# A layernorm, attention and FFN kernel in split precision: narrow matmuls joined, layernorm shared with GpSimd, eight idle transposes at the branch

## The chip, the cores and the metric

The kernel runs on one core of a Trainium2 chip. TensorE (PE) multiplies matrices into PSUM, an accumulator memory of eight banks; VectorE (DVE), ScalarE (ACT) and GpSimd (POOL) do elementwise work[...]; SyncE (SP) issues DMAs, as ACT and POOL also do. Each engine works through its own queue in order, and semaphores tie the queues together. The metric is the device time of one execution in microseconds, lower is better.

## What is computed

Four sequences of 512 tokens with 512 features pass a layernorm. Its output goes through causal attention with 16 heads of 128, and through a gated FFN whose three weight matrices hold -1, 0 and 1. The results are multiplied and added to x.

```python
xn = _layernorm(x)                                   # x: 4 x 512 x 512
q = einsum("bpd,hde->bphe", xn, W_Q) + b_Q           # k and v alike
scores = where(causal, einsum("bqhe,bkhe->bhqk", q, k) / sqrt(128), -1e5)
z = einsum("bkhe,bhqk->bqhe", v, softmax(scores))
s = einsum("bqhe,hed->bqd", z, W_O) + b_O
hdn = silu(einsum("th,ih->ti", xn, gate_w) * gate_s) * (einsum("th,ih->ti", xn, up_w) * up_s)
g = silu(einsum("ti,hi->th", hdn, down_w) * down_s)  # 1408 wide inside
out = x + s * g
```

## The kernel before

**Split precision.** Matmuls run in fp32r, whose operands are rounded. Each operand is therefore kept as a high part (ACT copies it with rounding) and a low part (the value minus the high part), a `Split`. A product is three matmuls into one PSUM bank: high x low, high x high, low x high (`mm3`).

**Stages.** A start loads x and the first weights, normalizes batch 0 and transposes it (128 x 128 transposes on TensorE). Then 64 heads run in an order of groups of two heads (`HG = 2`), the four batches inside each group. After them, one value says whether the FFN weights are exact in the high part alone, every engine branches on it, and `ffn` runs.

**One head `n`**, in the order in which its instructions are issued on every engine (the order is written out by hand):

1. `softmax`: scores of this head in three PSUM tiles, row maximum on DVE, exponent on ACT, reciprocal on DVE, scaling of p on GpSimd.
2. two `project_v` (first head of a pair) or two `project_out` of the group before (second head): `fill` over the first half of the tokens.
3. `turn_p`: p is transposed in 32 x 32 blocks on DVE, written to DRAM and read back with its blocks in place.
4. `split_p`: the p of the head before is split, in two halves, on ACT (high, `pth`) and DVE (low, `ptl`). In the first heads it comes before step 2.
5. `split_pending`: weights that are due are split, high on ACT, low on GpSimd. Weights are loaded through four `raw` buffers; later loads wait on the ACT queue until GpSimd has finished with a buffer.
6. `project`: q and k of the next head, each evacuated by ACT (high) and DVE (low).
7. `attend`: z of the head before, from twelve matmuls of 512, 128, 384 and 256 columns in three rounds. Key tile j of 128 reaches only query tiles j and later, so the last key tile has 128 columns. z is evacuated by ACT (`zT.hi`) and DVE (`zT.lo`).
8. `fill` over the second half of the tokens.

In heads 0, 2 and 4 the next batch is also normalized: statistics and `ln_normalize` on DVE, then in step 8 four `ln_transpose` (four transposes, a copy to the high part on ACT) and `ln_low` (DVE).

PSUM has three banks for score and transpose tiles (`ps_st`) and five for all else (`ps_mm`), reused in turn. `warm_up` issues 24 transposes of the identity at the start. The line in `softmax` that reads the high and low part of k side by side is

```python
nc.tensor.matmul(two, qT.hi[:, :P], kT.both[:, :, :P], start=True, stop=False)
nc.tensor.matmul(where[0], qT.lo[:, :P], kT.hi[:, :P], start=False, stop=True)
```

Of the kernel before, what the change touches and what calls it, by code (L numbers as in the profile page):

```python
# [10 lines left out]
F32 = mybir.dt.float32  # L11
F32R = mybir.dt.float32r
# [10 lines left out]
BIG = 3.0e38  # L23
WARM = 24
LOW_BITS = (1 << 12) - 1
# [17 lines left out]
def kernel(  # L43
# [46 lines left out]
    def mm3(ps, a, b, first, last):  # L90
        nc.tensor.matmul(ps, a.hi, b.lo, start=first, stop=False)  # L91
        nc.tensor.matmul(ps, a.hi, b.hi, start=False, stop=False)  # L92
        nc.tensor.matmul(ps, a.lo, b.hi, start=False, stop=last)  # L93


    with ExitStack() as at:
# [35 lines left out]

        def split_w(dst, raw):
            nc.scalar.copy(dst.hi, raw)
            nc.gpsimd.tensor_tensor(dst.lo, raw, dst.hi32, ALU.subtract)

# [12 lines left out]

        def split_pending(n):  # L150

            for due, dst, raw in [p for p in pending if p[0] <= n]:
                split_w(dst, raw)
            pending[:] = [p for p in pending if p[0] > n]
# [46 lines left out]

        def warm_up():

            junk = ps_st.tile([P, NT, P], F32, name="warm", tag="st")
            for k in range(WARM):
                nc.tensor.transpose(junk[:, k % NT, :], ident, ident)

        def ln_normalize(b, t):
            xt = x_in.pop((b, t))
            mv, sd = ln_of.pop((b, t))  # L210
            rstd = small.tile([P, 1], F32, name="rstd")
            nc.vector.reciprocal(rstd, sd)
            xn = lnp.tile([P, D], F32, name="xn")
            nc.vector.tensor_scalar(xn, xt, mv[:, 0:1], rstd, ALU.subtract, ALU.mult)
            xn_of[b, t] = xn

        def ln_transpose(b, t):
            xn = xn_of.pop((b, t))
            pool, tag = ((ps_st, "st"), (ps_mm, "mm"))[t % 2]
            tr = pool.tile([P, ND, P], F32, name="tr", tag=tag)  # L220
            for c in range(ND):
                nc.tensor.transpose(tr[:, c, :], xn[:, ts(c, P)], ident)
            to = xnT[b][:, :, ts(t, P)]
            nc.scalar.copy(to.hi, tr)
            lo_of[b, t] = lambda: nc.vector.tensor_tensor(to.lo, tr, to.hi32, ALU.subtract)  # L225

        def ln_low(b, t):
            lo_of.pop((b, t))()
# [3 lines left out]
        def project_v(g, b, t):  # L232
            ps = ps_mm.tile([P, HG * E], F32, name="psv", tag="mm")
            for c in range(ND):
                mm3(ps, xnT[b][:, c, ts(t, P)], wv[g][:, c, :], c == 0, c == ND - 1)
            v = weight(vp, [P, HG * E], f"v{g}_{b}_{t}", "v")
            nc.scalar.copy(v.hi, ps)
            nc.vector.tensor_tensor(v.lo, ps, v.hi32, ALU.subtract)
            v_of.setdefault((g, b), []).append(v)

        def project(b, h, w, bias, name, parts=1):

            ps = ps_mm.tile([P, S], F32, name="ps" + name, tag="mm")
            both = qkp.tile([P, 2, S], F32R, name=name, tag=name)
            q = Split(both[:, 0, :], both[:, 1, :])
            q.both = both
            for k in range(parts):
                at_ = ts(k, S // parts)
                for c in range(ND):
                    mm3(ps[:, at_], w[:, c, :], xnT[b][:, c, at_], c == 0, c == ND - 1)  # L250
                yield
                nc.scalar.activation(  # L252
                    q.hi[:, at_], ps[:, at_], AF.Identity, bias=bias[:, h : h + 1]
                )
                nc.vector.scalar_tensor_tensor(  # L255
                    q.lo[:, at_], ps[:, at_], bias[:, h : h + 1], q.hi32[:, at_],
                    ALU.add, ALU.subtract,
                )
            yield q
# [85 lines left out]

        def split_p(raw):
            pt = weight(pp, [P, NS, P], "pt", "pt")
            half = NQ // 2
            for k in range(0, NQ, half):
                src = raw[:, k : k + half].rearrange("p b (s i) -> p b s i", i=Q)  # L350

                def dst(part):
                    return part[:, :, k * Q : (k + half) * Q].rearrange(
                        "p s (b i) -> p b s i", i=Q
                    )

                nc.scalar.copy(dst(pt.hi), src)  # L357
                nc.vector.tensor_tensor(dst(pt.lo), src, dst(pt.hi32), ALU.subtract)  # L358
            return pt

        def transpose_p(of):

            pt = weight(pp, [P, NS, P], "pt", "pt")
            pairs = [(j, t) for j in range(NT) for t in range(j, NT)]
# [10 lines left out]

        def attend(h, pt, vs):
            z = ps_mm.tile([P, NT, P], F32, name="z", tag="mm")


            todo = []  # L380
            for part, other in (("hi", "hi"), ("lo", "hi"), ("hi", "lo")):
                for j in (0, NT - 1, 1, 2):
                    v = getattr(vs[j], part)[:, ts(h % HG, E)]
                    p_ = getattr(pt, other)[:, slot[j] : slot[j] + NT - j, :]
                    todo.append((z[:, j:, :], v, p_))
            for k, (o, v, p_) in enumerate(todo):
                nc.tensor.matmul(o, v, p_, start=k == 0, stop=k == len(todo) - 1)  # L387
            zT = weight(zp, [P, NT, P], f"z{h}", "z")

            bias = bv_sb[:, h : h + 1]  # L390
            nc.scalar.activation(zT.hi, z, AF.Identity, bias=bias)
            nc.vector.scalar_tensor_tensor(zT.lo, z, bias, zT.hi32, ALU.add, ALU.subtract)
            return zT
# [67 lines left out]
        with tc.manual_schedule():  # L461
            nc.gpsimd.memset(eps, EPS)
            for t in range(NT):
                load_x(0, t)
            prepare_qk(0, -4, -3)
            prepare_v(0, -2)
            bq_sb, bk_sb, bv_sb, gs_sb, us_sb = small_const()
# [7 lines left out]
            make_causal_mask(nc, mask[:, S - P :], mask_val=IGNORE / SCALE)  # L475
            ln_stats(0, [0])
            ln_sd(0, [0])
            ln_stats(0, [1])
            ln_sd(0, [1])
            ln_normalize(0, 0)  # L480
            split_pending(-4)
            ln_transpose(0, 0)
            ln_stats(0, [2])
            ln_sd(0, [2])
            ln_normalize(0, 1)
            ln_low(0, 0)
            split_pending(-3)
            ln_transpose(0, 1)
            ln_low(0, 1)
            q_of = project(0, 0, wq[0], bq_sb, "q", 2)  # L490
            k_of = project(0, 0, wk[0], bk_sb, "k", 2)
            next(q_of)
            split_pending(-2)
            prepare_qk(1, -1)
            ln_stats(0, [3])
            ln_sd(0, [3])
            ln_normalize(0, 2)
            ln_transpose(0, 2)
            ln_normalize(0, 3)
            ln_low(0, 2)  # L500
            ln_transpose(0, 3)
            next(k_of)
            ln_low(0, 3)
            next(q_of)
            next(k_of)
            split_pending(-1)
            table(AF.Exp)
            qT = next(q_of)
            kT = next(k_of)
            for t in range(NT):  # L510
                load_x(1, t)
            bo_bc = load_const(b_o.broadcast_to([P, D]), [P, D], "bo_bc")
            ds_bc = load_const(down_s.broadcast_to([P, D]), [P, D], "ds_bc")
            project_v(0, 0, 0)

# [5 lines left out]
            def attend_last(before, pt):  # L521
                g, b, i = before
                zs.setdefault((g, b), []).append(attend(g * HG + i, pt, v_of[g, b]))

            for n, (g, b, i) in enumerate(heads):
# [21 lines left out]
                if n == 1:  # L547
                    pt = split_p(raw)
                of = softmax(qT, kT)
                if n > 1 and early:  # L550
                    pt = split_p(raw)
                look()
# [4 lines left out]
                if not early:  # L557
                    pt = split_p(raw)
                split_pending(n)
# [24 lines left out]
                if nxt is not None:  # L584
# [7 lines left out]
                    if ln_next:  # L592
                        for t in range(NT):
                            ln_normalize(b + 1, t)
                if nxt is not None:
# [6 lines left out]
                if ln_b is not None and n > 0:  # L602
                    ln_sd(ln_b, range(NT))
                    table(AF.Exp)
                if ln_next:
                    fill(range(half, NT))
                    for t in range(NT):
                        ln_transpose(b + 1, t)
                        ln_low(b + 1, t)
                    if b + 2 < B:  # L610
                        for t in range(NT):
                            load_x(b + 2, t)
# [10 lines left out]
            last = (NG - 1, B - 1)  # L623
            zs[last].append(attend(H - 1, pt, v_of[last]))
            for t in range(NT):
                project_out(*last, t, zs[last])


# [175 lines left out]
```

## Time and profile before

| what | us |
|---|---|
| three runs, median (lowest to highest) | 1222.99 (1222.97 to 1223.63) |
| the profiled execution | 1222.41 |
| its span, first to last instruction | 1220.6 |
| first score matmul | 20.58 |
| last matmul of the attention starts | 972.68 |
| first FFN matmul starts | 974.00 |
| last matmul ends, near | 1213.9 |

Busy time by stretch, in us:

| stretch | length | PE | DVE | ACT | POOL |
|---|---|---|---|---|---|
| 20.58 to 95.48, first heads | 74.90 | 72.55 | 65.35 | 44.81 | 14.11 |
| 228.98 to 243.90, one head, n = 14 | 14.92 | 14.92 | 12.46 | 7.43 | 5.61 |
| 243.90 to 258.57, the next | 14.67 | 14.67 | 12.32 | 8.06 | 8.71 |
| 258.57 to 964.80, the other heads | 706.23 | 706.23 | 523.87 | 323.01 | 180.28 |
| 973.08 to 1213.90, the FFN | 240.82 | 239.90 | 96.49 | 68.77 | 45.90 |

A row of the timeline reads: start in us, length in us, engine, line, operation, output<-inputs, shape (partitions x elements), count, and in brackets the idle time before it and what ended it. `L387` is line 387 of the kernel before. PE stands for the matmuls, PEld for the loads of their stationary operand. A row of waits reads: engine, tile and line that waited, who was waited for, total us, times, longest. A row by stretch reads: stretch, length, then busy time and count of PE, PEld, DVE, ACT and POOL, then the granted TensorE clock, the share of the DMA engines and GB/s.

### The profile page before, as it was taken

How to read it: one execution, taken by the hardware profiler on the slowest of the kernel's cores; microseconds unless marked ns; L12 is line 12 of the kernel's file. 1: busy time of each engine (PE TensorE's matmuls, PEld its weight loads, DVE VectorE, ACT ScalarE, POOL GpSimd, SP SyncE). 2: the span in 40 equal slices, each digit the busy share in tenths (PEclk: the TensorE clock that was granted, in tenths of full speed). 3: DMA queues.
4: the chain of work that ended last, by engine and by line, in shares of the span. 5: the costliest groups of instructions: out<-in, count | busy, mean ns of one | idle time of the engine just before them, and what ended most of it. 6: DMA issues, size and time to landing. Idle time of an engine off the chain costs nothing.

```text
span 1220.6 us, 18887 instructions
## 1 busy us (share of the span) xinstructions
PE 1206.5 (99%) x6514; PEld 1052.7 (86%) x6514; DVE 827.1 (68%) x2044; ACT 525.3 (43%) x1169; POOL 301.7 (25%) x433
## 2 busy tenths in 40 slices
PE   8999999999999999999999999999999999999997
PEld 8888888888888888888888888888888888888886
DVE  6897777777777777777877676767677533434343
ACT  5654444444445445444544454445444342323231
POOL 4212321232123213321412141214121341212010
PEclk9999999999999999999999999999999999999999
DMA  4454456656665667566655565555544893627241
GB/s 161 138 175 147 145 165 206 206 179 190 190 207 174 203 198 218 181 208 192 211 182 173 178 189 175 177 185 173 173 156 156 272 317 93 207 87 213 80 147 38
DMA packets 117912, 215.55 MB, mean 177 GB/s; under 512 B 13232, under 2 KB 45744, under 8 KB 117808
## 3 DMA queue, kind: packets, MB, share of 16 engines
q1 hardware_dynamic: 74016, 134.51, 34.4%
q10 hardware_dynamic: 29376, 53.26, 14.2%
q0 software_dynamic: 14416, 26.48, 7.9%
q8 instruction: 53, 0.87, 0.3%
q14 instruction: 51, 0.42, 0.1%
HBM read 135.17 MB, written 79.04 MB: 175 GB/s over the span
## 4 chain that ended last, share of the span: by engine, by line
PE 95%; DVE 3%; ACT 1%; DMA 0%; issue 0%; SPq 0%; DVEq 0%; ACTq 0%
PE z L387 10%; PE pd L667 7%; PE pg L667 7%; PE pu L667 7%; PE pso L91 5%; PE psv L91 5%; PE pso L92 5%; PE pso L93 5%; PE psv L93 5%; PE psv L92 5%; PE psq L91 5%; PE psq L92 5%; PE psq L93 5%; PE psk L91 5%; PE psk L92 5%; PE psk L93 5%
## 5 line engine op out<-in xcount | busy, mean ns | idle before, releaser
L316 POOL TENSOR_SCALAR p<-p,rtot 128x512 f32<-128x512 f32 (+3 forms) x256 | 148.2, 598 | 675.1 <-DVE rtot L315 675.1
L312 ACT ACTIVATE p<-p,nmax 128x512 f32<-128x512 f32 (+3 forms) x256 | 140.9, 552 | 147.3 <-DVE nmax L298 147.3
L358 DVE TENSOR_TENSOR ptl<-ptr,pth 128x640 fp32r<-128x640 f32 x126 | 133.7, 1099 | 1.4 <-ACT pth L357 1.4
L330 DVE STREAM_TRANSPOSE sq<-p 128x256 f32<-128x256 f32 x378 | 113.3, 361 | 0.0
L298 DVE CUSTOM_DVE_ANT_0 p<-sc,mask 128x512 f32<-128x512 f32 (+2 forms) x192 | 96.5, 552 | 0.3 <-PE sc L93 0.3
L252 ACT ACTIVATE k<-psk,consts 128x512 fp32r<-128x512 f32 (+1 forms) x65 | 44.2, 681 | 108.7 <-PE psk L93 108.6
L252 ACT ACTIVATE q<-psq,consts 128x512 fp32r<-128x512 f32 (+1 forms) x65 | 44.3, 682 | 97.2 <-PE psq L93 72.6
L357 ACT CAST pth<-ptr 128x640 fp32r<-128x640 f32 x126 | 84.9, 724 | 0.1
L413 DVE TENSOR_TENSOR a<-pso,a 128x512 f32<-128x512 f32 x108 | 72.1, 686 | 17.7 <-PE pso L93 16.4
L255 DVE SCALAR_TENSOR_TENSOR k<-psk,consts,k 128x512 fp32r<-128x512 f32 (+1 forms) x65 | 48.0, 739 | 52.8 <-ACT k L252 52.7
L693 DVE SCALAR_TENSOR_TENSOR hd<-pu,consts,sg 128x512 f32<-128x512 f32 x44 | 33.0, 751 | 66.8 <-PE pu L667 62.2
L315 DVE RECIPROCAL rtot<-tot 128x1 f32<-128x1 f32 x256 | 41.6, 162 | 42.7 <-ACT p L312 36.3
L91 PE MATMUL sc<-k,q 128*128 128x512 f32 (+2 forms) x192 | 65.7, 342 | 1.7 <-DVE xl L225 1.7
L93 PE MATMUL sc<-k,q 128*128 128x512 f32 (+2 forms) x192 | 64.7, 337 | 0.0
L92 PE MATMUL sc<-k,q 128*128 128x512 f32 (+2 forms) x192 | 64.7, 337 | 0.0
L255 DVE SCALAR_TENSOR_TENSOR q<-psq,consts,q 128x512 fp32r<-128x512 f32 (+1 forms) x65 | 47.6, 732 | 7.6 <-ACT q L252 7.6
L312 ACT ACTIVATION_READ_ACCUMULATOR p<-p,nmax 128x1 f32 x256 | 47.8, 187 | 0.0
L91 PEld LDWEIGHTS sc<-k,q 128*128 128x128 f32 x192 | 36.2, 188 | 7.9 <-DVE xl L225 3.5
L723 ACT ACTIVATE o<-o 128x512 f32<-128x512 f32 (+1 forms) x17 | 10.3, 607 | 68.8 <-DVE o L722 68.8
L92 PEld LDWEIGHTS sc<-k,q 128*128 128x128 f32 x192 | 36.2, 189 | 3.6
L93 PEld LDWEIGHTS sc<-k,q 128*128 128x128 f32 x192 | 36.1, 188 | 2.6
L691 ACT ACTIVATE sg<-pg,consts 128x512 f32<-128x512 f32 x44 | 30.3, 688 | 17.0 <-PE pg L667 17.0
(734 smaller groups left out, 3811.6 us busy)
## 6 DMA issues: line engine op xcount, KB each, us to landing
turn<-sq SPq DMA_DIRECT2D x63, 640.0 KB, 3.8
ptr<-turn SPq DMA_DIRECT2D x252, 160.0 KB, 3.4
acc<-a SPq DMA_DIRECT2D x124, 256.0 KB, 3.7
a<-acc ACTq DMA_DIRECT2D x108, 256.0 KB, 2.8
xt<-in_x SPq DMA_DIRECT2D x16, 256.0 KB, 4.1
wor<-in_w_o ACTq DMA_DIRECT2D x16, 256.0 KB, 4.5
fa<-acc SPq DMA_DIRECT2D x16, 256.0 KB, 5.9
fx<-in_x SPq DMA_DIRECT2D x16, 256.0 KB, 6.9
```

The costliest lines, as they stand in the source:

```text
L91: nc.tensor.matmul(ps, a.hi, b.lo, start=first, stop=False)
L92: nc.tensor.matmul(ps, a.hi, b.hi, start=False, stop=False)
L93: nc.tensor.matmul(ps, a.lo, b.hi, start=False, stop=last)
L252: nc.scalar.activation(q.hi[:, at_], ps[:, at_], AF.Identity, bias=bias[:, h : h + 1])
L255: nc.vector.scalar_tensor_tensor(q.lo[:, at_], ps[:, at_], bias[:, h : h + 1], q.hi32[:, at_], ALU.add, ALU.subtract,)
L298: nc.vector.tensor_tensor_reduce(out=of[t], in0=where[t], in1=add, scale=-SCALE, scalar=BIG, op0=ALU.add, op1=ALU.min, accum_out=nmax[t],)
L312: nc.scalar.activation(of[t], of[t], AF.Exp, bias=nmax[t], scale=-1.0, accum_out=tot)
L316: nc.gpsimd.tensor_scalar(of[t], of[t], rtot, 1.0, ALU.mult, ALU.mult)
L330: nc.vector.transpose(dst.rearrange("p a s i -> p s a i"), src.rearrange("p (s a i) -> p s a i", s=n, i=Q),)
L358: nc.vector.tensor_tensor(dst(pt.lo), src, dst(pt.hi32), ALU.subtract)
L387: nc.tensor.matmul(o, v, p_, start=k == 0, stop=k == len(todo) - 1)
L667: nc.tensor.matmul(ps, l, r, start=first and k == 0, stop=last and k == len(pairs) - 1)
```

## The change

Seven edits come together.

- **Joined z.** In heads 9 to 60 the last key tile leaves the three rounds. Its products go to a PSUM tile of their own, `z2`: one matmul of 256 columns over the high and low part of p side by side, and one of 128. The two halves of `z2` are added to the last part of z on DVE. p's split is one tile with both parts.
- **Split of p.** In heads 9 to 61 the low part of the first half of p is made by GpSimd.
- **Order in a projection.** `project_v` and `project` issue all high x high matmuls first, then those with one operand's low part, then those with the other's (`mm3_all`); each half of the first q and k has its own PSUM tile.
- **Transposes among the matmuls.** In heads 0, 2 and 4 the layernorm transposes of the next batch are issued one by one between the matmuls of `project_v` (`side`).
- **Normalizing on GpSimd.** `ln_normalize` of later batches, and of tiles 2 and 3 of the first, runs on GpSimd.
- **Start.** Weights of q and k are loaded ahead of x tiles 2 and 3; the first halves of q and k, the first `project_v` and the second halves follow in another order; low parts of the first v weights are made on DVE; 20 warm-up transposes instead of 24.
- **Branch.** Eight transposes of the identity (`LINGER`) follow the last `project_out`.

```diff
-WARM = 24
+WARM = 20
+LINGER = 8
...
+    def mm3_all(ps, pairs):
+        todo = [
+            (getattr(a, i), getattr(b, k))
+            for i, k in (("hi", "hi"), ("lo", "hi"), ("hi", "lo"))
+            for a, b in pairs
+        ]
+        for n, (l, r) in enumerate(todo):
+            nc.tensor.matmul(ps, l, r, start=n == 0, stop=n == len(todo) - 1)
+            if side:
+                side.pop(0)()
...
-            nc.vector.tensor_scalar(xn, xt, mv[:, 0:1], rstd, ALU.subtract, ALU.mult)
+            on.tensor_scalar(xn, xt, mv[:, 0:1], rstd, ALU.subtract, ALU.mult)
...
-                nc.vector.tensor_tensor(dst(pt.lo), src, dst(pt.hi32), ALU.subtract)
+                on = nc.gpsimd if shared and k == 0 else nc.vector
+                on.tensor_tensor(dst(pt.lo), src, dst(pt.hi32), ALU.subtract)
...
-                for j in (0, NT - 1, 1, 2):
+                for j in range(last) if joined else (0, last, *range(1, last)):
...
+            if joined:
+                z2 = ps_mm.tile([P, 2, P], F32, name="z2", tag="mm")
+                nc.tensor.matmul(z2, vs[last].hi[:, e], pt.both[:, :, s_, :], start=True, stop=False)
+                nc.tensor.matmul(
+                    z2[:, 0], vs[last].lo[:, e], pt.hi[:, s_, :], start=False, stop=True
+                )
...
+            if not joined:
+                leave(slice(0, NT), z)
+                return zT
+            leave(slice(0, last), z[:, :last])
+            rest = small.tile([P, 2, P], F32, name="rest", bufs=1)
+            nc.scalar.copy(rest, z2)
+            nc.vector.tensor_tensor(rest[:, 0], rest[:, 0], rest[:, 1], ALU.add)
+            nc.vector.tensor_tensor(rest[:, 1], z[:, last], rest[:, 0], ALU.add)
+            leave(last, rest[:, 1])
             return zT
...
-            for t in range(NT):
-                load_x(0, t)
+            load_x(0, 0)
+            load_x(0, 1)
             prepare_qk(0, -4, -3)
+            load_x(0, 2)
+            load_x(0, 3)
             prepare_v(0, -2)
...
-            ln_stats(0, [0])
-            ln_sd(0, [0])
-            ln_stats(0, [1])
-            ln_sd(0, [1])
+            for t in range(2):
+                ln_stats(0, [t])
+                ln_sd(0, [t])
             ln_normalize(0, 0)
+            ln_normalize(0, 1)
+            ln_stats(0, [2])
             split_pending(-4)
             ln_transpose(0, 0)
-            ln_stats(0, [2])
+            ln_transpose(0, 1)
+            ln_low(0, 0)
+            ln_low(0, 1)
             ln_sd(0, [2])
...
+            ln_stats(0, [3])
+            ln_sd(0, [3])
+            table(AF.Exp)
+            ln_normalize(0, 2, nc.gpsimd)
+            ln_normalize(0, 3, nc.gpsimd)
+            split_pending(-2, nc.vector)
+            prepare_qk(1, -1)
             q_of = project(0, 0, wq[0], bq_sb, "q", 2)
             k_of = project(0, 0, wk[0], bk_sb, "k", 2)
             next(q_of)
...
+            next(k_of)
             ln_transpose(0, 2)
+            ln_transpose(0, 3)
             ln_low(0, 2)
...
+            project_v(0, 0, 0)
             next(q_of)
             next(k_of)
...
                     if ln_next:
                         for t in range(NT):
-                            ln_normalize(b + 1, t)
+                            ln_normalize(b + 1, t, nc.gpsimd)
...
                 if ln_next:
+                    for t in range(NT):
+                        side.extend(ln_transposes(b + 1, t))
+                        side.append(lambda t=t: ln_low(b + 1, t))
                     fill(range(half, NT))
-                    for t in range(NT):
-                        ln_transpose(b + 1, t)
-                        ln_low(b + 1, t)
+                    while side:
+                        side.pop(0)()
...
             for t in range(NT):
                 project_out(*last, t, zs[last])
+            warm_up(LINGER)
```

## The prediction

> **What bounds the kernel now.** I read the busy shares first, then who waited for whom on TensorE, then stretches of time, then the start times of single matmuls.
>
> ```profile
> span 1220.6 us, 18887 instructions
> PE 1206.5 (99%) x6514; PEld 1052.7 (86%) x6514; DVE 827.1 (68%) x2044; ACT 525.3 (43%) x1169; POOL 301.7 (25%) x433
> ...
> PE psq L91 <- DVE xl L225: 2.1, 1, 2.1
> PE sc L91 <- DVE xl L225: 1.7, 4, 0.6
> PE warm L206 <- POOL ident masks.py:199: 1.4, 1, 1.4
> PE pg L667 <- PE pso L93: 0.9, 1, 0.9
> PE tr L222 <- DVE k L255: 0.7, 1, 0.7
> PE psq L91 <- DVE q L255: 0.4, 1, 0.4
> ```
>
> TensorE is idle for 14.1 of 1220.6 us. Those six rows are its only waits on others (7.2 us), in the start, in the first five heads, and one at the branch before the second half; 5.6 us more lie after its last matmul. From 258.57 to 964.80 us the table of stretches has it busy for 706.23 of 706.23 us. In steady state only fewer or shorter matmuls make the kernel faster, and another engine costs something only once it is late enough to stop TensorE.
>
> A busy row says nothing of a matmul's price, since the ends are modelled; the distance between starts does:
>
> ```profile
> 505.45 0.39 PE L387 MATMUL z<-pth,v_0h 128*128 128x512 f32 x1
> 505.68 0.22 PE L387 MATMUL z<-pth,v_3h 128*128 128x128 f32 x1
> 505.73 0.39 PE L387 MATMUL z<-pth,v_1h 128*128 128x384 f32 x1
> 505.96 0.28 PE L387 MATMUL z<-pth,v_2h 128*128 128x256 f32 x1
> 506.08 0.40 PE L387 MATMUL z<-pth,v_0l 128*128 128x512 f32 x1
> ...
> 526.48 0.28 PE L289 MATMUL sc<-k,q 128*128 128x256 f32 x1
> 526.60 0.22 PE L290 MATMUL sc<-k,q 128*128 128x128 f32 x1
> 526.66 0.34 PE L91 MATMUL psv<-wv4l,xh 128*128 128x256 f32 x1
> 526.83 0.28 PE L92 MATMUL psv<-wv4h,xh 128*128 128x256 f32 x1
> ```
>
> The narrow z matmul occupies 0.05 us itself, but the 384 behind it then takes 0.23 instead of its usual 0.173 (three in 0.52 us in the scores). A narrow matmul is too short to hide the next weight load, so it costs nearly as much as a 256-wide one. L289/L290 already do what the change does: one 256-wide matmul over the high and low parts side by side, then one narrow.
>
> **Two pages of the skill.** The Trainium skill, "TensorE: Matmul & The Clock Gate", Part 4, says a transpose does not count as TensorE activity for the clock. Against this trace:
>
> ```profile
> 1.41 5.38 PE L206 MATMUL warm<-ident 128*128 128x128 f32 x24 [1.41 <-POOL ident masks.py:199]
> 8.20:10.20 2.00, 0.00 (x0) 0.00 (x0) 1.39 (x3) 2.00 (x6) 2.00 (x2) 1.00 0.04 15
> 10.20:12.60 2.40, 2.35 (x12) 2.36 (x13) 2.29 (x6) 0.60 (x2) 2.40 (x3) 0.58 0.75 224
> ```
>
> The 24 warm-up transposes take 0.22 us each to the last; 16 late ones take 1.66 us (93.82 to 95.48), 0.104 each. The first q matmuls, from 10.25 us, go at 0.21 per 256 columns; the fast pace of 0.12 comes only after some 14.1 us, 3.8 us after real matmuls began. (The clock column, third from the end, reads 1.00 before there is a record.) Page and trace agree, so I give idle transposes no clock gain. "GPSIMD Engine Reference", section 8, says GpSimd shares its SBUF interfaces with VectorE, with contention for VectorE instructions that have two SBUF inputs. Here:
>
> ```profile
> 236.31 3.56 DVE L358 TENSOR_TENSOR ptl<-ptr,pth 128x640 fp32r<-128x640 f32 x2
> 237.32 1.88 POOL L135 TENSOR_TENSOR wk4l<-wkr,wk4h 128x512 fp32r<-128x512 f32 x1
> ```
>
> Alone the pair takes 1.52 us (518.04) and the GpSimd subtract 1.29. They agree, and I go by these rows.
>
> **Part by part**, against the profiled execution: span 1220.6 of 1222.41 us, 0.58 below the 1222.99 median. I apply the same difference to the median.
>
> *Joined z, heads 9 to 60: 52 heads.* Pitches: 512 wide 0.2267 (eight pg in 1.81), 384 0.173, 256 0.120 (twelve psv in 1.44). Three rounds of 512+384+256 are 1.558 of the 1.91 us, so three narrow matmuls cost 0.352, 0.117 each. They give way to one 256 (0.120) and one narrow last. That narrow one, read from the score block, costs 0.121 before a psv (26 heads) and 0.134 before a pso (26). Saved: 26 x 0.111 + 26 x 0.098 = **5.4 us**. The high and low parts now lie 1280 elements apart within one read; L289 reads so over 512 at no extra price; bound 0 to 5.9 us in all.
>
> *Its evacuation* turns one ACT and one DVE step into three and four: ACT 0.69 becomes about 0.56+0.42+0.39, DVE 0.75 about 0.6+0.25+0.29+0.29 (nearest rows: v_0h, v_0l, add, p of 128). The chain goes ACT, DVE, ACT, DVE and ends some 2.5 us after z instead of 1.6. Queued behind it on ACT are the v copies, on DVE the v and pso evictions and the next softmax, some 0.5 us later. Who waits: the next pso of this z, 4.6 us after it (507.4 to 512.0), so the margin is 2 us; k.lo stands ahead of z's steps in both queues, and the score banks are written again only a head later. Cost nothing. The extra PSUM tile makes seven of five buffers per head; the tightest reuse, the pso after a psv head's scores on z's bank, comes about 5 us after z. No wait.
>
> *Half of ptl to GpSimd.* VectorE loses one 0.76 (1.78 with contention). GpSimd takes 640/512 x 1.29 = 1.6 us, up to 2.4 with strides and contention, behind p's scaling (2.49) and ahead of the weight splits. In the head at 228.98 us it runs 234.9 to 236.5; its reader, z's third pass, starts at 240.1: margin 3.6. What it pushes: wq and wk splits, and ACT's two weight loads that wait for their buffers (239.23), behind which ACT's q and k wait. k.lo ended at 242.15 and the next scores start at 243.90: margin 1.75 against a shift of 0.5 to 1.2, in six heads. Cost nothing.
>
> *Startup.* SP loads wq and wk before x tiles 2 and 3 (two issues of 0.45 earlier); four warm-ups fewer let the first transpose start with xn, near 6.0 instead of 6.6. Both transposes end near 7.7; xh of tile 1 follows wq.hi and xh of tile 0 on ACT and ends near 8.5. With high parts first, q starts there instead of at 10.25, since x.lo (9.3) is needed only by the last four matmuls. Twelve slow ones: to 11.0. k needs wk.hi (9.4) and wk.lo (10.7, GpSimd): six slow (to 12.3, release 3.8 us after 8.5), six fast: 13.05. xn 2 and 3 on GpSimd queue behind wk.lo: 10.7 to 11.9. Transposes to 13.9, v to 15.3 (wv.hi waits for the Exp table, 13.1; wv.lo, now DVE, 14.0), second halves of q and k to 18.2, then nothing covers k: ACT 0.45, DVE 0.48, first scores near 19.3 against 20.58. **Gain 1.3 us**; bounds -0.5 to 2.8, since landing times and the clock's release are inferred. The next q/k weight loads move later on SP's queue, ahead of batch 1's x; these are first read near 25.7 and have 10 us.
>
> *Layernorm in the heads (n = 0, 2, 4).* DVE sheds 4 x 0.55; GpSimd takes near 0.69 each (p's 512-wide row) and delivers at about the same times. But TensorE now meets the first transpose right behind the first psv instead of after 24. 24 psv and 16 transposes are 4.5 us. At n = 0 xn comes at 31.55 in the old timing, so scores end near 37.4 against 37.29: +0.1. At n = 2 xn comes at 59.6: end 65.8 against 65.99, the waits of 0.56 and 0.41 on xl being gone. At n = 4 xn is there: -0.25. Together **-0.35**; bounds -1.2 to +1.5.
>
> *Eight transposes at the branch.* 8 x 0.104 = 0.83 behind the last pso; the 0.92 us of "issue" that follow there show no releaser, and nothing says they overlap. The first pg matmuls already go at 0.23, so there is no clock to win. **+0.85**; bounds 0 (the gap swallows them) to 1.8 (sequencing on top).
>
> The same number of projection matmuls in another order costs nothing: each loads its weights before and after.
>
> Sum: -5.4 - 1.3 - 0.35 + 0.85 = -6.2: profiled 1216.2, median **1216.8**.
>
> **Rivals.** (a) *The join saves nothing*: the strided read or the exposed load eats it. For it: only two rows show such pairs; against: both show full pace. -0.8: 1222.2. (b) *Slower: GpSimd's half becomes the wait.* TensorE stops at z's third pass in each of 52 heads once that half takes over 5.2 us (1.6 plus 3.6 margin). Against a 6.2 us gain the sign turns at 5.3 us, and a measurable loss of 2.4 us needs 5.4; at 5.5 us: 52 x 0.3 = 15.6 lost, 1232.4. For it: three producers share GpSimd and a contended VectorE subtract already more than doubles; against: GpSimd's own worst subtract is 1.88. (c) *The start gives nothing* and layernorm stalls add 1.5: -5.4+1.5+0.85: 1219.9, still faster.
>
> **Chances.** The bound for no change is 0.2%, 2.4 us. Forecast with its small variations 0.70, (c) 0.13, (a) 0.07, (b) 0.10. Range 1214.0 to 1220.2: the bounds of start, layernorm and branch around 1216.8, reaching to (c); (a) and (b) are left out. Faster 0.82, same 0.08, slower 0.10.
>
> **What would show it.** z's block at 1.80 instead of 1.91 us, no TensorE wait on ptl or z in steady state; first scores near 19.3; pg starting 0.8 us later behind the last pso. Wrong if a TensorE wait on GpSimd's ptl or on k.lo appears in many heads, or if the matmul after the joined pair is delayed by more than 0.06 us.

## The result, and the profile after

| | median, us | runs | lowest to highest |
|---|---|---|---|
| before | 1222.98 | 6 | 1222.11 to 1223.63 |
| changed | 1233.03 | 6 | 1232.48 to 1234.76 |

The ratio is 1.0085 (95% interval 1.0072 to 1.0098): the change costs 10 us where 6 were forecast as a gain. The profiled execution took 1232.81 us, its span is 1230.9, 10.3 more than before. Its page, and TensorE's waits:

```profile
span 1230.9 us, 19243 instructions
...
PE 1205.4 (98%) x6466; PEld 1051.6 (85%) x6466; DVE 785.5 (64%) x2135; ACT 550.1 (45%) x1273; POOL 405.7 (33%) x498
```

```profile
PE tr L247 <- POOL xn L230: 13.4, 9, 4.1
PE warm L222 <- POOL ident masks.py:199: 1.4, 1, 1.4
PE sc L92 <- DVE k L280: 1.1, 1, 1.1
PE psq L104 <- ACT xh L249: 0.7, 1, 0.7
...
```

TensorE's own busy time is lower than before, as meant, and VectorE was relieved of 42 us. But a row that did not exist now leads the waits: TensorE stood nine times, 13.4 us in all, before a transpose until GpSimd had normalized its tile. There is no wait on the low half of pt and none on z. The list by tile says what GpSimd takes for one tile, and what VectorE takes (ns: lowest, median, highest; then the first and last start):

```profile
L230 POOL TENSOR_SCALAR xn<-xt,mv,rstd x14: 2057/2069/2077, 10.9 to 106.9; 128x512 f32<-128x512 f32 x14
L230 DVE TENSOR_SCALAR xn<-xt,mv,rstd x2: 546/546/546, 5.4 to 6.0; 128x512 f32<-128x512 f32 x2
```

2.07 us, three times the 0.69 that the forecast went by. The timeline of the first layernorm head (n = 0), with some of its rows:

```profile
31.74 8.24 POOL L230 TENSOR_SCALAR xn<-xt,mv,rstd 128x512 f32<-128x512 f32 x4 [4.72 <-DVE rstd L228]
...
33.87 0.33 PE L247 MATMUL tr<-ident,xn 128*128 128x128 f32 x1 [3.66 <-POOL xn L230]
...
35.92 0.47 PE L247 MATMUL tr<-ident,xn 128*128 128x128 f32 x1 [0.61 <-POOL xn L230]
...
36.41 0.41 PE L247 MATMUL tr<-ident,xn 128*128 128x128 f32 x1
```

The four tiles come 2.06 us apart until 39.98, and the transposes, set between psv matmuls, follow at GpSimd's pace. The table of stretches shows the second part of the loss; here are the three layernorm heads (n = 0, 2, 4), from marker to marker, after and then before. The marker of a head is the start of its 256-wide score matmul. Columns: us, busy time and instructions of TensorE, its weight loads, VectorE, ScalarE, GpSimd; granted clock; DMA share; GB/s.

```profile
22.80:43.76 20.96, 16.69 (x89) 14.70 (x88) 12.69 (x41) 10.96 (x23) 12.42 (x11) 0.84 0.46 138
52.97:77.86 24.89, 20.15 (x114) 17.88 (x113) 15.76 (x46) 12.20 (x27) 12.81 (x10) 0.86 0.44 122
92.53:112.03 19.50, 17.32 (x114) 15.49 (x112) 12.27 (x37) 9.32 (x21) 10.29 (x8) 1.00 0.32 99
```

```profile
22.16:37.11 14.95, 14.26 (x89) 12.11 (x88) 13.93 (x44) 10.72 (x23) 2.05 (x4) 1.00 0.55 173
46.62:65.81 19.19, 17.57 (x113) 15.28 (x112) 16.81 (x48) 11.74 (x27) 4.61 (x6) 1.00 0.40 111
80.47:97.47 17.00, 16.95 (x113) 15.40 (x112) 14.22 (x40) 9.04 (x21) 2.05 (x4) 1.00 0.37 113
```

The length less TensorE's busy time is its idle time: 4.27 us against 0.69, 4.74 against 1.62, 2.18 against 0.05, together 8.8 us more. The busy time for the same work rose as well, by 2.4, 2.6 and 0.4 us: in the first two heads the granted clock fell to 0.84 and 0.86 of full. Finer stretches of the changed kernel show when:

```profile
38.00:40.00 2.00, 2.00 (x10) 1.86 (x9) 1.11 (x2) 0.90 (x3) 1.98 (x1) 0.50 0.38 133
40.00:42.00 2.00, 2.00 (x12) 1.97 (x12) 0.69 (x1) 0.56 (x2) 0.00 (x0) 0.60 0.48 131
42.00:44.00 2.00, 2.00 (x15) 1.87 (x15) 1.59 (x3) 1.99 (x4) 0.00 (x0) 1.00 0.02 8
```

Stretches of 0.05 us put the beginning at 34.8 and the end at 41.6 us: soon after the 3.66 us stop TensorE works at half its clock for 6.8 us (the transposes of 0.41 us above, 0.27 is their usual duration). At n = 4, where no single stop is longer than 0.81 us, the clock stays at 1.00. The markers cut the whole difference into places:

| stretch | before | changed | difference |
|---|---|---|---|
| start to the marker of n = 0 | 22.16 | 22.80 | +0.64 |
| n = 0 to n = 5 (three layernorm heads) | 75.31 | 89.23 | +13.92 |
| n = 5 to n = 63 (joined z) | 858.57 | 852.64 | -5.93 |
| n = 63 to the end of VectorE's last step | 259.69 | 259.65 | -0.04 |
| from there to the end of the span | 4.87 | 6.58 | +1.71 |
| sum | | | +10.30 |

So nothing went wrong in the steady state. The z block there, in the timeline of the changed kernel:

```profile
504.37 0.28 PE L424 MATMUL z<-pt,v_3h 128*128 128x256 f32 x1
504.49 0.22 PE L425 MATMUL z<-pt,v_3l 128*128 128x128 f32 x1
504.55 0.45 PE L92 MATMUL pso<-wo3l,z6h 128*128 128x512 f32 x1
504.84 0.40 PE L93 MATMUL pso<-wo3h,z6h 128*128 128x512 f32 x1
```

The joined matmul takes 0.12, the narrow one 0.06, and the 512 behind it starts its successor 0.29 later instead of 0.23: 0.24 us for the pair.

### The profile page after: what moved, and what is told of

Same layout as the page of the kernel before. It is cut to its first block, busy times and chain, and to the rows that moved or that the text cites. A ratio compares the mean times of both kernels' runs of the same rounds, so it can differ in the third digit from the quotient of the medians.

```text
span 1230.9 us, 19243 instructions
## 1 busy us (share of the span) xinstructions
PE 1205.4 (98%) x6466; PEld 1051.6 (85%) x6466; DVE 785.5 (64%) x2135; ACT 550.1 (45%) x1273; POOL 405.7 (33%) x498
## 4 chain that ended last, share of the span: by engine, by line
PE 94%; DVE 2%; POOL 1%; issue 1%; DMA 1%; ACT 1%; SPq 0%; POOLq 0%; DVEq 0%; ACTq 0%
PE psv L104 15%; PE psq L104 13%; PE psk L104 13%; PE z L421 8%; PE pd L726 7%; PE pg L726 7%; PE pu L726 6%; PE pso L92 5%; PE pso L93 5%; PE pso L94 5%; PE sc L92 3%; PE sc L93 3%; PE sc L94 3%; POOL xn L230 1%; PE tr L247 1%
## 5 line engine op out<-in xcount | busy, mean ns | idle before, releaser
L389 POOL TENSOR_TENSOR pt<-ptr,pt 128x640 fp32r<-128x640 f32 x53 | 83.5, 1576 | 9.4 <-ACT pt L387 9.2
L387 ACT CAST pt<-ptr 128x640 fp32r<-128x640 f32 x126 | 85.0, 724 | 0.1
L467 DVE TENSOR_TENSOR a<-pso,a 128x512 f32<-128x512 f32 x108 | 69.4, 681 | 0.1
L339 DVE RECIPROCAL rtot<-tot 128x1 f32<-128x1 f32 x256 | 41.6, 163 | 42.7 <-ACT p L336 36.3
L389 DVE TENSOR_TENSOR pt<-ptr,pt 128x640 fp32r<-128x640 f32 x73 | 66.7, 924 | 1.4 <-ACT pt L387 1.4
L421 PE MATMUL z<-pt,v_0h 128*128 128x512 f32 x128 | 50.5, 395 | 0.0
L421 PE MATMUL z<-pt,v_1h 128*128 128x384 f32 x128 | 44.2, 345 | 0.0
L782 ACT ACTIVATE o<-o 128x512 f32<-128x512 f32 (+1 forms) x17 | 10.3, 607 | 68.8 <-DVE o L781 68.8
L92 PEld LDWEIGHTS sc<-k,q 128*128 128x128 f32 x192 | 36.2, 188 | 5.2 <-DVE k L280 1.3
```

The source lines that it names most:

```text
L389: on.tensor_tensor(dst(pt.lo), src, dst(pt.hi32), ALU.subtract)
```

## The experiments

The theory after the result: GpSimd's normalization is the whole loss; with it undone, join and start give what was forecast. Its rival: cutting the transposes into steps between psv matmuls costs TensorE, whoever normalizes.

**Normalization back on VectorE, in all places and in the heads alone.**

```
e1_norm_on_vector:
-            ln_normalize(0, 2, nc.gpsimd)
-            ln_normalize(0, 3, nc.gpsimd)
+            ln_normalize(0, 2)
+            ln_normalize(0, 3)
-                            ln_normalize(b + 1, t, nc.gpsimd)
+                            ln_normalize(b + 1, t)
e2_norm_heads_vector: the last of these edits only
```

> The changed kernel with every layernorm normalization back on VectorE, interleaved transposes kept. Theory A (the loss is GpSimd's 2.07 us per normalized tile, which TensorE meets at the first transposes, and the halved clock behind that stall): the stalls at heads 0, 2 and 4 all but go, first scores near 19.3 us, scores of head 5 near 97 us instead of 112, total 1216 to 1218.5. Theory B (the interleaving itself stops TensorE, since it meets a transpose before the first tile is normalized whoever does it): stalls of some 2 us stay at heads 0 and 2 with a halved clock behind them, total 1222 to 1226.

> As e1, but tiles 2 and 3 of the first batch stay on GpSimd. Theory A: first scores stay near 21.1 us as in the changed kernel, heads 0 to 5 as in e1, so 1.5 to 2 us above e1. Theory B: as e1 within 0.5 us, since the start would not be the place.

The first: median 1218.71 us, ratio 0.9974 (0.9964 to 0.9984). That is 3.5 us below the kernel before, timed beside it, and 14.3 below the changed kernel, beside which the kernel before read 0.8 us more. The second: 1221.53 in one run, span 1219.8 against 1216.7. From n = 0 to n = 5 they take 77.11 and 77.13 us, so the two GpSimd tiles at the start cost some 2.7 us on their own (n = 0 at 23.08 against 20.37; kernels with the same start differ by up to 1.6 us there, so this is rough), the twelve in the heads about 12. The rival has a small share, 1.8 us, since before took 75.31 there. In the first of the two kernels:

```profile
PE tr L247 <- DVE xn L230: 4.4, 2, 2.4
```

```profile
58.00:60.00 2.00, 1.58 (x8) 1.58 (x9) 1.89 (x7) 0.00 (x0) 0.00 (x0) 0.66 0.75 310
60.00:62.00 2.00, 2.00 (x12) 2.00 (x10) 2.00 (x4) 0.61 (x2) 0.00 (x0) 0.50 0.41 110
```

The first transpose now stands behind a single psv matmul, comes up before VectorE has its tile, and the stop of 2.40 us that ends at 58.42 is followed by half clock.

**GpSimd kept, interleaving undone; and the instruction cut in two.**

```
e4_norm_gpsimd_not_interleaved:
-                    for t in range(NT):
-                        side.extend(ln_transposes(b + 1, t))
-                        side.append(lambda t=t: ln_low(b + 1, t))
...
-                    while side:
-                        side.pop(0)()
+                    for t in range(NT):
+                        ln_transpose(b + 1, t)
+                        ln_low(b + 1, t)
e5_norm_two_instructions, on GpSimd:
-            on.tensor_scalar(xn, xt, mv[:, 0:1], rstd, ALU.subtract, ALU.mult)
+                on.tensor_scalar(xn, xt, mv[:, 0:1], 1.0, ALU.subtract, ALU.mult)
+                on.tensor_scalar(xn, xn, rstd, 1.0, ALU.mult, ALU.mult)
```

> The changed kernel with the transposes behind the matmuls of project_v again, normalization on GpSimd kept. Theory A: TensorE has 24 psv matmuls (2.9 us) to do while GpSimd works, but the fourth tile still comes 8.2 us after the first began, so only 1 to 2 us per head come back: 1228 to 1230. Theory B: the whole loss in the heads goes: 1218 to 1220.

> The changed kernel with the GpSimd normalization as two instructions, subtract of the mean and then multiplication by rstd, each with one per-partition operand and a constant 1.0. If the price of 2.07 us is that of two per-partition operands in one instruction: each of the two takes near the 0.6 to 0.7 us of p's 512-wide row, 1.2 to 1.4 per tile, and the total falls by 6 to 9 us to 1224 to 1227. If it is the subtract's price: the first takes 1.4 or more, the sum stays near 2 us and the total within 1 us of the changed kernel's.

The first gave 1234.87 us; from n = 0 to n = 5 it takes 89.70 us, against 89.23 with the interleaving. (Its n = 0 comes at 24.39, after a stop of 2.41 us and half clock from 16.4 to 20.0, so the total is higher still.) The gain of the order that was expected isn't there: TensorE still ends each of these heads when the fourth tile comes. The second gave 1242.53 us, for the two instructions together take 2.70 us a tile, more than either expectation allowed. The list by tile shows where the 2.07 us sit:

```profile
L231 POOL TENSOR_SCALAR xn<-xt,mv x14: 1997/2002/2942, 10.6 to 115.9; 128x512 f32<-128x512 f32 x14
L232 POOL TENSOR_SCALAR xn<-xn,rstd x14: 694/696/700, 12.7 to 118.0; 128x512 f32<-128x512 f32 x14
```

The multiply by a value per partition costs what the forecast's row said. The whole price is in the instruction with the subtract.

**The subtract, written otherwise.** Two forms keep the changed kernel's plan and order, and let VectorE make one value per partition for it:

```
e7_mult_add:
+                nc.vector.tensor_scalar(nb, mv[:, 0:1], rstd, -1.0, ALU.mult, ALU.mult)
+                on.tensor_scalar(xn, xt, rstd, nb, ALU.mult, ALU.add)
e12_add_mult:
+                nc.vector.tensor_scalar(nb, mv[:, 0:1], -1.0, None, ALU.mult)
+                on.tensor_scalar(xn, xt, nb, rstd, ALU.add, ALU.mult)
```

> The changed kernel with GpSimd's normalization written as x times rstd plus nb, where nb = -mean*rstd is made by VectorE, instead of x minus mean times rstd. Theory A (the subtract operation is what costs 2.0 us on GpSimd; the multiply took 0.69): GpSimd's xn near 0.7 us in place of 2.06, the waits for it nearly gone, span near 1217 to 1219. Rival (two operands by partition in one instruction cost it, or an add costs what a subtract does): xn near 2 us and a span near 1231.

> The changed kernel with GpSimd's normalization as x plus nb times rstd, where nb = -mean is made by VectorE: the same two operands by partition and the same order of the two operations as in the changed kernel, with an add in place of the subtract. Theory A (the subtract is what costs 2.06 us): xn on GpSimd near 0.77 us, span near 1218. Rival (a first operation that is not a multiply costs, or the order): xn near 2 us, span near 1231.

They took 1220.31 and 1219.99 us (one run each). The instruction of the second differs from the changed kernel's in an add of -mean for a subtract of mean, and in that -mean has a tile of its own, while the mean is a column of `mv`:

```profile
L233 POOL TENSOR_SCALAR xn<-xt,nb,rstd x14: 754/763/772, 10.0 to 92.9; 128x512 f32<-128x512 f32 x14
```

0.76 us against 2.07, with the same two operands per partition and the same sequence of operations. So the form with the subtract is what GpSimd does slowly, and the plan to share the layernorm did not fail on GpSimd as such. (Every slow form here also reads the column of `mv`, and no fast one does; no run separates the two. VectorE reads the same column and subtracts in 0.55 us.) But even so it is no gain: from n = 0 to n = 5 these two take 78.34 and 79.32 us, more than before's 75.31, because the interleaved transposes still stop TensorE twice in each (5.6 and 5.2 us in all).

**VectorE alone and no interleaving; the same without the branch matmuls; the join alone.**

```
e6_dve_noside: the edits of the first and of the fourth experiment above together
e8_noside_nolinger: and
-            warm_up(LINGER)
e9_join_alone, on the kernel before:
-            pt = weight(pp, [P, NS, P], "pt", "pt")
+            pt = p_split()
...
+                nc.tensor.matmul(z2, vs[last].hi[:, e], pt.both[:, :, s_, :], start=True, stop=False)
...
+            rest = small.tile([P, 2, P], F32, name="rest", bufs=1)
```

> The changed kernel with all four tiles of the normalization on VectorE and with the three later layernorm heads no longer cut into steps between score matmuls; the eight matmuls at the branch are kept. Theory A (the loss was GpSimd's normalization alone, and interleaving adds one small stall, 2.4 us at head 2): about 2 us below the version with all normalization on VectorE and the interleaving, whose span was 1216.7, so a span near 1214 and a median near 1217; heads 0, 2 and 4 then grow as in the kernel before, less 0.11 each for the joined matmul. Theory B (interleaving is a gain that GpSimd's stall covered): span 1218 or more.

> As the version with VectorE alone and no interleaving, and also without the eight matmuls at the branch. Theory A (they lie inside the branch gap, 1.32 us from the last score-side matmul to the first feed-forward one without them, 1.37 with them): that gap near 1.32, the time within 0.3 us of its twin, the stretch behind the branch equal. Rival (my forecast's figure): 0.85 us faster without them.

> The kernel before with only the joined z matmul and its one weight tile for the last keys, nothing of the layernorm, the start or the branch. Theory A (the join saves on TensorE what the pitch of the markers says, 0.11 us a head over some 52 heads): ratio 0.9952, near 1217. Rival (the 5.9 us read from the markers is made by the shifted phase of the heads and not by the join): within 1 us of before, or slower.

| | median, us | ratio to before | n = 0 at | n = 0 to 5 | n = 7 to 63 |
|---|---|---|---|---|---|
| VectorE, not interleaved | 1215.91 | 0.9944 (0.9928 to 0.9961) | 20.02 | 75.38 | 824.23 |
| and no branch matmuls | 1215.46, one run | | 19.65 | 75.32 | 823.12 |
| join alone | 1216.83 | 0.9952 (0.9936 to 0.9969) | 22.26 | 75.37 | 823.10 |
| before | | | 22.16 | 75.31 | 828.95 |

Without the interleaving the layernorm heads are those of before to 0.07 us, so the order gains nothing and costs 1.7 us with VectorE (77.11). The join alone saves 5.85 us between n = 7 and n = 63 and 5.5 in the median; its pt has high and low parts in one tile, with the low half all VectorE's, and its pitch equals that of the kernels which share it with GpSimd, so the sharing is worth nothing either way. In the first row one head, n = 30, is some 1.1 us longer than in the others, and so it is in the run without warm-up below, but not in its twin here. The timeline of that head, with some of its rows:

```profile
470.32 1.87 POOL L151 TENSOR_TENSOR wk8l<-wkr,wk8h 128x512 fp32r<-128x512 f32 x1
...
472.23 0.34 ACTq L146 DMA_DIRECT2D wkr<-in_w_k  x1
472.59 1.57 ACTq L492 DMA_DIRECT2D look<-in_up_w  x1
474.21 0.69 ACT L279 ACTIVATE q<-psq,consts 128x512 fp32r<-128x512 f32 x1 [5.30 <-PE z L425]
...
475.74 0.74 PE L104 MATMUL psv<-wv3h,xh 128*128 128x256 f32 x4 [0.83 <-DVE q L280]
```

This is the chain that the forecast watched: GpSimd splits a weight, ScalarE then issues the load that needs its buffer, and q stands behind it. GpSimd's half of pt pushes it: from the marker of the head, the split of wk ends after 9.25 us here, and after 8.64 in the join alone, where VectorE makes both halves. But the larger part is that ScalarE took 1.57 us to issue the next load (1.58 in the run without warm-up, 0.46 in the changed kernel and in the join alone). A psv matmul then waited 0.83 us for VectorE's step on q. Why that issue is slow in two executions stays open.

Behind n = 63 the first two rows take 265.96 and 265.99 us to the end of the span, so the eight branch matmuls cost nothing that can be seen. The changed kernel's timeline at the branch says why:

```profile
981.24 0.39 PE L94 MATMUL pso<-wo7h,z15l 128*128 128x512 f32 x1
981.47 1.03 PE L222 MATMUL warm<-ident 128*128 128x128 f32 x8
982.61 0.47 PE L726 MATMUL pg<-xl,wg0h 128*128 128x512 f32 x1
```

From the last pso to the first pg it is 1.37 us with them; before it is 1.32 (972.68 to 974.00). They lie in a gap that is there anyway.

**The start without warm-up**, and the best version timed:

```
e10_warm0, on the version without branch matmuls:
-WARM = 20
+WARM = 0
e11_join_and_start: that version unchanged, timed five times
```

> The version with VectorE alone, no interleaving and no matmuls at the branch, and now also no warm-up matmuls at the very start (20 before). Theory T (transposes raise the granted clock as other matmuls do): the eight transposes at 6.05 us then are TensorE's first work, the first q matmuls at 8.0 run at the slow pitch of 0.21 us, as in the kernel before, until some 4 us after the transposes began, and the first head's marker comes 0.3 to 1.2 us later than 19.65. Theory S (transposes don't count, as the Trainium skill says in TensorE: Matmul & The Clock Gate): the first q matmuls run as they did with the warm-up, 0.12 to 0.15 us apart from 8.0 on, and the marker stays at 19.65.

> The same text as the version with VectorE alone, no interleaving and no matmuls at the branch, now timed in five rounds: the joined matmul and the new start are what is left of the change. Sum of the parts by the markers: -5.7 (join) and -2.5 (start), with some 1.5 us given back after the last VectorE instruction, so near 1215.7, ratio 0.9945. Rival (the start's gain is all lost before the end): as the join alone, 0.9952 or above.

TensorE's timeline with the warm-up (the version without branch matmuls), and then without it:

```profile
1.41 4.05 PE L222 MATMUL warm<-ident 128*128 128x128 f32 x20 [1.41 <-POOL ident masks.py:199]
...
6.05 1.31 PE L247 MATMUL tr<-ident,xn 128*128 128x128 f32 x8 [0.60 <-DVE xn L230]
...
8.04 0.74 PE L104 MATMUL psq<-xh,wq0h 128*128 128x256 f32 x4 [0.68 <-ACT xh L249]
...
8.62 0.64 PE L104 MATMUL psq<-xh,wq0l 128*128 128x256 f32 x4
```

```profile
8.65 1.23 PE L104 MATMUL psq<-xh,wq0h 128*128 128x256 f32 x4 [0.68 <-ACT xh L249]
9.68 1.05 PE L104 MATMUL psq<-xh,wq0l 128*128 128x256 f32 x4
10.53 1.05 PE L104 MATMUL psq<-xl,wq0h 128*128 128x256 f32 x4
...
13.09 0.87 PE L104 MATMUL psk<-xl,wk0h 128*128 128x256 f32 x4
```

With 20 warm-up transposes the second group of four starts 0.58 us after the first and the third 0.48 after that: full pace from the first matmul on. Without them a group takes 0.85 us, 0.21 a matmul, until some 13.3 us, and n = 0 comes at 21.91 instead of 19.65; the time was 1219.22 in its one run. Transposes do raise the clock here; the slow stretch even outlasted the expected end by 3 us. The kernel before has the same in its trace. There the first eight transposes run ahead of any other matmul but the warm-up, and their weight loads go from 0.21 us each to 0.105, the pace of the late ones:

```profile
6.38 0.85 PEld L222 LDWEIGHTS tr<-ident,xn 128*128 128x128 f32 x4
7.44 0.42 PEld L222 LDWEIGHTS tr<-ident,xn 128*128 128x128 f32 x4 [0.21 <-DVE xn L214]
```

The join alone, which has the start of before, is at that pace from 6.12 us on, runs its first q matmuls at 0.12 us after a stop of 1.99 us, and falls to half clock only at 11.2 us.

The best version took 1215.85 us, ratio 0.9945 (0.9932 to 0.9959), below both kernels and near the sum of its parts. Its n = 0 came at 20.80 in the profiled execution: with the same text, a late load of an x tile (VectorE waited 1.17 us for it at 7.87) moved the start by 1.15 us.

## Why the prediction was wrong

The step that failed is a term of the layernorm sum: "GpSimd takes near 0.69 each (p's 512-wide row) and delivers at about the same times". The row was a multiply of one operand; the instruction here subtracts first, and took 2.07. Four of them are 8.3 us in a head where 2.8 were counted. The bounds given for that step, -1.2 to +1.5 us, were drawn from the schedule alone and held the price itself fixed, though the profile of before had no such instruction. Even its own dearer GpSimd rows (1.29 and 1.88 for a subtract of the same size, already in the text for another step) would have opened the range to the slow side. The Trainium skill, "GPSIMD Engine Reference", section 4.1, puts operations with one tensor input at roughly VectorE's rate. The multiply (0.69) and the add (0.76) beside VectorE's 0.55 come near that; the subtract's 2.07 does not, and the measurement decides. The forecast also had no term for the clock behind a stop: in the three heads 8.8 us are added idle time, and 5.4 are added busy time for the same work, 5.0 of them in the two heads at half clock.

- **Layernorm, -0.35 forecast, +13.92 measured.** The forecast did name what makes this possible, that the first transpose stands behind one psv instead of 24: cover was given up in the same edit that made the producer slower. With VectorE normalizing it still costs 1.7, without the interleaving it costs 0.
- **Start, -1.3 forecast, +0.64 measured.** Two errors of opposite sign. Tiles 2 and 3 came at 12.95 and 15.01 instead of 11.9 (the same price; TensorE waited 0.84 and 1.40). And "twelve slow ones" with "release 3.8 us after 8.5" was wrong: the first q matmuls ran at full pace. With VectorE normalizing, the first marker came 1.4 to 2.5 us earlier than before in four executions (20.80, 20.37, 20.02, 19.65), so the forecast was on the low side of what the start can give. The statement it leaned on, that of the Trainium skill, "TensorE: Matmul & The Clock Gate", Part 4, that transposes don't count for the clock, had seemed to agree with the trace of before: 24 slow warm-ups, then slow q matmuls. The forecast passed over the transposes between them, of which the last four went at full pace, and over the stop of 2.15 us behind those (8.10 to 10.25). It took the slow pace for proof that the transposes had done nothing. With a stop of 0.68 us in the same place the q matmuls are fast, and without the warm-up they are slow.
- **Join, -5.4 forecast, -5.93 measured** by the markers, -5.5 in the median of the join alone: right, and by its mechanism. The pair costs 0.24 us where three cost 0.352, and the matmul behind it is late by just the 0.06 that the text allowed.
- **Evacuation and GpSimd's half of pt at no cost: right for the changed kernel.** TensorE waits for neither in any head; the half took 1.58 us on average where 1.6 was said. The margin is thin, though: in two later executions the chain behind it cost 1.1 us in one head.
- **Branch, +0.85 forecast, +0.05 measured.** The lower bound, "the gap swallows them", is what happened.
- **The end**, which was not in the sum: from VectorE's last step to the end of the span it is 4.87 us before, 5.56 with the join alone and 6.25 to 6.97 in the kernels with the changed start. What the extra time is was not found, and it stays open. (The forecast put 5.6 us behind the last matmul of before; from 1213.9 to the end of the span they are 6.7.)

Rival (b) gave 1232.4, close to the 1233.03 measured, and was wrong: GpSimd did become what TensorE waits for, but for xn in three heads, not for pt in 52. A time that fits is no evidence for its mechanism; the row of the waits is.

## What to carry to other kernels

Before an elementwise step moves to another engine, look for a row with the same operations on that engine; if there is none, its price is unknown by a factor and belongs in the range on the bad side, and a form that is known to be cheap (here an add of the negated value) can be tried. Don't in one edit make a producer slower and move its consumer ahead of the work that covered it. On a matrix engine that is always busy, the saving of a narrow matmul can be read from the distance between starts, and it comes out as computed.

## What the runs showed of the hardware

- GpSimd, 128x512 float32 with values per partition: multiply 0.69 us, multiply then add 0.77, add then multiply 0.76, subtract then multiply 2.00 to 2.07 (always with the mean from a column of `mv`). VectorE's subtract then multiply takes 0.55.
- Transposes against the identity bring TensorE to full clock: with 20 of them the first q matmuls go at 0.12 us, without them at 0.21 for 4.7 us.
- A stop of TensorE can cost more than its length. Behind stops of 3.66 and 4.06 us it ran at half clock for 6.8 us, behind one of 2.40 for 3.4. The Trainium skill, "TensorE: Matmul & The Clock Gate", section "Why this matters for your kernels", warns of gaps over about 3 us. Here shorter ones sometimes do it: half clock followed one of 1.99 us (join alone) and did not follow one of 2.62 (first layernorm head of the multiply-then-add form). With GpSimd normalizing and no interleaving, half clock came from 37.0 to 47.4 in a head whose four stops were of 0.91 to 1.40 us. The same page's Part 1 says that the activity window runs freely, which would make it depend on where the stop falls. No run here shows the window itself, but the spells come in steps: by stretches of 0.05 us, 3.4 us in three runs (10.55 to 14.0 in the kernel before, 11.2 to 14.65 in the join alone, 58.6 to 62.05 with VectorE normalizing) and 6.8 twice in the changed kernel (34.75 to 41.6, 68.9 to 75.75).
